# One core, a two-layer graph network: denominators on 32 columns, an earlier mask and a new order of groups

## The chip, the cores and the metric

The kernel runs on one core of one Trainium2 chip. The metric is the device time of one execution in microseconds (us). TensorE (PE) multiplies matrices, with the weights loaded by a second stream (PEld); VectorE (DVE) and ScalarE (ACT) work element by element; GpSimd (POOL) does small element work and issues the gathers; SyncE (SP) issues the plain DMAs. Each engine and each DMA queue takes its instructions in the order in which they were built.

## The reference

The input is `x` (32 images x 512 nodes x 256 features, f32) and `adj` (32 x 512 x 512, 0 or 1, about 3% ones). Two layers follow, each a graph step and then a feed-forward step, with a layer norm ahead of each and a residual sum after it.

```
L0 graph   h = x W_msg;  out = relu(x W_upd + (adj^T h) / max(degree, 1) + bias)
L0 ffn     t = max over d of (x[d] + Wt[:, d]) + bt          # 1024 features, "tropical"
           trop = piecewise linear function of t;  cls = gelu(x Wc + bc);  g = sigmoid(x Wg + bg)
           out = (g * trop + (1 - g) * cls) Wd + bd
L1 graph   four heads of 64:  h = x W[head]
           w[i, j] = leaky_relu(src[i] + dst[j]) where adj[i, j] is 1, else minus infinity
           out = softmax over j of w[i, j], times h;  relu, + h, layer norm per head
L1 ffn     softmax over 64 slices per head of 8; tokens = weighted sums of x over the nodes / weights' sum;
           a short state-space scan over the 64 tokens, forwards and backwards; back to nodes; out projection
```

## The kernel before

The large matmuls are in f32. In the profile one f32 matmul of the program is two TensorE instructions, a transpose is one. P = 128 partitions, N = 512 nodes, NT = 4 tiles of 128 nodes, D = 256.

**The built order.** The code is a set of generators. Every `yield` ends a step, and `woven(a, na, b, nb)` takes steps of two generators in the ratio na : nb. The building layer may still move an instruction in its engine's order where nothing depends on it, so the order on each engine is fixed when the program is built. Tiles come from rings (`bufs`); a tile that takes the place of an older one waits until that one's last reader is done.

**L0** (`layer0_sorted`). The images are cut into 4 segments of 8. `convs` runs the graph step of a segment image by image (`conv_in`, `conv_out`: names `ph`, `pu`, `pm`, `lnpa`), then `put_in_order` sorts the segment's 4096 nodes by how many of their largest features can matter for the tropical maximum. Beside the first segment, `features` sorts the 1024 feed-forward features by the shape of their function: it scatters rows to DRAM, loads them back in order (`wraw`, `fld`, `wd`) and turns them on TensorE (`wtp`, L358) into `table` and the weights. The sorted nodes are 32 tiles of 128 with caps 24, 9, 7, 6, 5, 5, 5, then five of 4, four of 3, seven of 2, nine of 1: a tile with cap k gathers one row of `table` per node as a start (`best`) and k - 1 more (`rows`, L576), and takes the maximum on VectorE (L579). Group g of a segment holds tiles g, g + 8, g + 16 and g + 24. `sums(s, g)` is that gathering; `mixed(s, g)` is the classical product, gate and piecewise function (`clsp`, `gatep`, L599; `tz`, L606; L601 to L617); `down(s, g)` is the last product (`po`, L626) and the store to `x2s`. `feed_forwards` runs the first group's `sums` alone and then weaves `mixed` of a group with `sums` of the next; all of it is woven with the convolutions of the next segment (`ahead`), which end with the set-up of L1's constants.

**L1** (`layer1_plain`). For image b, `prepare(b)` gathers x, loads `adj` (`ai`), makes `a` (bf16) and two sums per row on ScalarE (L1102, L1103), turns `a` on TensorE (`maskp`, L1160) and copies it to `mask` (L1161); it norms and turns x (`x3T`), forms the heads (`hp`, L1131) and three factors of the weights; one of them, `own`, is written to DRAM and read back as a row on all partitions for each head (L1151). `weigh` makes the weights of two heads and one j-tile on VectorE: `att` = max(own, other) * mask (L1170). `attention(b)` then has 8 turns: a pair of heads q (outer loop) and a tile j of 128 source nodes (inner loop). A turn multiplies `att` with the heads' values (numerator, `avp`) and with the column of `hv` that holds the factor of the denominator, broadcast to 64 columns (`adp`):

```
for dst, col, n in ((pv, 0, HO), (pd, HO, 1)):
    for k in range(2):
        h = 2 * q + k
        vals = hv[:, j, h, col : col + n]
        nc.tensor.matmul(dst[k * HO : (k + 1) * HO, :], vals if n > 1 else vals.to_broadcast([P, HO]),
                         weighed[b, h, j], start=j == 0, stop=j == NT - 1)
```

At the end of a pair ScalarE copies both sums from PSUM (L1215, L1216), and a turn later `back` transposes them (`dp`, `bp`, L1185) and divides on VectorE (L1187 to L1189). `norm` finishes the image inside the next image's turns.

`mixer(g)` does the feed-forward step of two images: `slices` (`x4T`; the logits `lgp`, L1289; the softmax; the token sums `yTp`, L1301; `swp`, L1306, whose copies add up `rn`), `tokens` (`uTp`, L1320, and `rnp`, L1323), `scan`, `unslice` (`outp`, L1518). Each `yield n` of the mixer earns n * PACE steps of `ahead`, the attentions with `prepare` of the image after them; WANTED is the sum of the n in one group, and TURNS and STEPS count the steps of an attention and a `prepare`. So attention work stands between the mixer's steps, and the numbers at the yields say how much of it stands where.

Of the kernel before, what the change touches and what calls it, by code (L numbers as in the profile page):

```python
# [96 lines left out]
def layer0_sorted(tc, ident, eps, x, adj, w, x2s, ranks, over, following):  # L97
# [29 lines left out]
    with ExitStack() as ctx:  # L127
# [80 lines left out]
        def features(raw):  # L208
# [141 lines left out]
            nc.sync.dma_start(wd, placed[:, :, D : 2 * D])  # L350
            wtT = rtile("wtT", [P, DC, FFN])
# [169 lines left out]
        def feed_forwards():  # L521
# [110 lines left out]
            groups = [(s, g) for s in range(len(x2s)) for g in range(NG)]  # L632
# [22 lines left out]
        with tc.tile_pool(name="r0", bufs=1) as raw:  # L655
            first = iter(lambda: next(ahead), 0)
            next(first)
            bounds(raw)
            for _ in woven(first, SEG * 10, features(raw), 50):
                pass  # L660
# [175 lines left out]
def layer1_plain(tc, ident, eps, x2s, ranks, adj, w, out, over, ps):  # L836
# [23 lines left out]
    TURNS = AP * (NT + 1) + 3  # L860
    STEPS = 15
    WANTED = 62
    AHEAD = 3
    ATT = 2 * (AHEAD + 2)
# [6 lines left out]
    with ExitStack() as ctx:  # L871
# [167 lines left out]

        yield True  # L1040
# [38 lines left out]
        def prepare(b):  # L1079
# [10 lines left out]
            a, raw = [], []  # L1090

            def load(t):
                raw.append(sb.tile([P, N], I32, tag="ai", name=f"ai{b}_{t}", bufs=2))
                nc.sync.dma_start(raw[t], adj[b, t * P : (t + 1) * P, :])

            load(0)
            load(1)
            yield
            for t in range(NT):
                n = b * NT + t  # L1100
                a.append(sb.tile([P, N], BF16, tag="a", name=f"a{b}_{t}", bufs=3))
                nc.scalar.activation(a[t], raw[t], AF.Identity, accum_out=edges[:, 0, n : n + 1])  # L1102
                nc.scalar.activation(raw[t], raw[t], AF.Square, accum_out=edges[:, 1, n : n + 1])  # L1103
                if t + 2 < NT:
                    load(t + 2)
                if t == 1:
                    mask = sb.tile([P, NT, N], BF16, tag="mask", name=f"mask{b}")
                    yield
                if t:
                    turn_edges(b, t - 1, a[t - 1], mask)  # L1110
                    yield
                if t == 2:

                    hv = sb.tile([P, NT, AH, HE], F32, tag="hv", name=f"hv{b}")
                    xn = hv.rearrange("p t h e -> p (t h e)")[:, : NT * D].rearrange("p (t d) -> p t d", t=NT)
                    normed(xt, xn, f"c{b}")
                    nc.gpsimd.tensor_add(xt, xt, beta.unsqueeze(1).to_broadcast([P, NT, D]))
                    yield
            turn_edges(b, NT - 1, a[NT - 1], mask)
            yield  # L1120
# [28 lines left out]
            own = [wide("own", f"own{b}_{h}", AH + 1) for h in range(AH)]  # L1149
# [6 lines left out]

        def turn_edges(b, t, a, mask):
            pt = ps.tile([P, NT, P], BF16, tag="any", name=f"maskp{b}_{t}")
            for j in range(NT):
                nc.tensor.transpose(pt[:, j, :], a[:, j * P : (j + 1) * P], identb)  # L1160
            nc.vector.tensor_copy(mask[:, :, t * P : (t + 1) * P], pt)  # L1161
# [11 lines left out]
        def attention(b):  # L1173

            mask, ht, hv, other, own = ready[b]
            xt = xs[b]
            av = sb.tile([P, NT, AH, HO], F32, tag="av", name=f"av{b}", bufs=1)
            turns = [(q, j) for q in range(AP) for j in range(NT)]

            def back(q, vT, dT):  # L1180

                bt, dt = psum("pv", f"bp{b}_{q}"), psum("pv", f"dp{b}_{q}")
                for src, dst in ((dT, dt), (vT, bt)):
                    for t in range(NT):
                        nc.tensor.transpose(dst[:, t * P : (t + 1) * P], src[:, t * P : (t + 1) * P], ident)  # L1185
                rs = sb.tile([P, NT, 2], F32, tag="rs", name=f"rs{b}_{q}")
                nc.vector.tensor_scalar_max(rs, dt.rearrange("p (t h e) -> p t h e", t=NT, h=2)[:, :, :, 0], 1e-30)  # L1187
                nc.vector.reciprocal(rs, rs)
                nc.vector.tensor_mul(av[:, :, 2 * q : 2 * q + 2, :], bt.rearrange("p (t h e) -> p t h e", t=NT, h=2),  # L1189
                                     rs.unsqueeze(3).to_broadcast([P, NT, 2, HO]))  # L1190

            def begin(b):
                if b < B and (b, 0, 0) not in weighed:
                    for q, j in turns[:AHEAD]:
                        weigh(b, q, j)

            begin(b)
            behind = None
            for i, (q, j) in enumerate(turns):
                if j == 0:  # L1200
                    pv, pd = psum("pv", f"avp{b}_{q}"), psum("pv", f"adp{b}_{q}")
                if i + AHEAD < len(turns):
                    weigh(b, *turns[i + AHEAD])

                for dst, col, n in ((pv, 0, HO), (pd, HO, 1)):
                    for k in range(2):
                        h = 2 * q + k
                        vals = hv[:, j, h, col : col + n]
                        nc.tensor.matmul(dst[k * HO : (k + 1) * HO, :], vals if n > 1 else vals.to_broadcast([P, HO]),  # L1209
                                         weighed[b, h, j], start=j == 0, stop=j == NT - 1)  # L1210
                for k in range(2):
                    weighed[b, 2 * q + k, j] = None
                if j + 1 == NT:
                    vT, dT = wide("att", f"avT{b}_{q}", ATT), wide("att", f"adT{b}_{q}", ATT)
                    nc.scalar.copy(dT, pd)  # L1215
                    nc.scalar.copy(vT, pv)  # L1216
                    behind = q, vT, dT
                yield
                if unfinished and i != 2:
                    next(unfinished[0], None)  # L1220
                    yield
                    if i > 2:
                        unfinished.pop()
                if j == 0 and behind:
                    back(*behind)
                    behind = None
                    yield
            if b + 1 in ready:
                begin(b + 1)
            back(*behind)  # L1230
            yield
            unfinished.append(norm(b, av))
# [39 lines left out]
        def slices(b, j, yT, rn):  # L1272
# [12 lines left out]
            yield 1  # L1285
            for t in range(NT):
# [10 lines left out]
                yield 4 if t + 1 == NT else 1  # L1297
# [14 lines left out]
        def tokens(g, yT, rn, uT):  # L1312
# [3 lines left out]
            for k in range(KC):  # L1316
                for i in range(P // C):
                    half, h = slice(i * C, (i + 1) * C), k * (P // C) + i
                    for c in range(DC):
                        nc.tensor.matmul(uv[half, k], wfxT[:, c, h * C : (h + 1) * C], yT[:, c, h],  # L1320
                                         start=c == 0, stop=c == DC - 1)
                    for j in range(GB):
                        nc.tensor.matmul(nv[half, k, j, :], rn[:, j, k : k + 1].to_broadcast([P, C]), ident[:, half],  # L1323
                                         start=True, stop=True)
# [9 lines left out]
        def scan(g, uT):  # L1334
# [123 lines left out]
            yield 6  # L1458
# [65 lines left out]
        def mixer(g):  # L1524
# [6 lines left out]
            yield 2  # L1531
# [659 lines left out]
```

## Time and profile before

| | us |
|---|---|
| median of three timed runs | 4762.39 (4759.25 to 4769.2) |
| profiled execution | 4746.8 |
| its span, first to last instruction | 4745.1 |
| first `clsp` of L0's first group | 352 |
| end of L0's last `po` | 2530 |
| first `avp` of L1 | 2565 |
| first and last group's `uTp` begin | 2683 and 4672 |

The profile is of one execution. Busy time of an engine is the union of its instructions' spans; a wait is idle time of an engine, put down to what ended it. In a row of groups stand the line, the engine and operation, the tiles written and read, the shape (for a matmul rows*columns of the array that it uses, then the output's shape), the count, then busy us, mean ns of one, idle us ahead of it and what ended that. A matmul's span holds its latency; how fast matmuls follow each other is read from their starts. Mean granted TensorE clock: 0.95.

### The profile page before, as it was taken

The page shows a single profiled execution, that of the slowest core. Times are in us where ns is not written, and L with a number is a line of the kernel's source. Part 1 is how long each engine was busy: PE and PEld are TensorE (multiplying, and loading weights), DVE is VectorE, ACT ScalarE, POOL GpSimd, SP SyncE. Part 2 cuts the span into 40 slices and gives each one's busy share as a digit, 9 for nine tenths or more (in the row PEclk, how much of TensorE's full clock was granted, in tenths as well). Part 3 has the DMA queues.
Part 4 walks back from the last instruction along what each step waited for, and adds up shares of the span by engine and source line. Part 5 has one row for each costly group of instructions (what it writes and reads, how often), then busy time and mean ns, then how long its engine had stood idle before and what let it go on. Part 6 is the DMA issues. An engine that isn't in the chain of part 4 may idle for free. (4 is left out here: it accounts for less than half of the span.)

```text
span 4745.1 us, 56724 instructions
## 1 busy us (share of the span) xinstructions
PE 4179.0 (88%) x19415; PEld 2594.1 (55%) x19415; DVE 3403.5 (72%) x7296; ACT 2325.0 (49%) x4852; POOL 1701.6 (36%) x2027
## 2 busy tenths in 40 slices
PE   5666989888998899889997999999999999999997
PEld 4444555555555565555554555555555555555555
DVE  6568778887787877777766877667676776666773
ACT  2335555455554556555655544444444444444432
POOL 2356443554435544353323222222222222222220
PEclk8878999999999999989998999999999999999999
DMA  4456443554335543464322111111111111111100
GB/s 122 158 186 197 136 130 113 193 177 134 121 125 179 184 131 115 124 230 158 121 90 83 38 48 54 50 45 54 49 41 39 45 56 50 54 45 50 43 10 19
DMA packets 235104, 474.12 MB, mean 100 GB/s; under 512 B 38300, under 2 KB 114076, under 8 KB 234805
## 3 DMA queue, kind: packets, MB, share of 16 engines
q0 software_dynamic: 80256, 282.38, 18.7%
q1 hardware_dynamic: 154548, 188.02, 12.5%
q8 instruction: 155, 2.54, 0.2%
q14 instruction: 145, 1.18, 0.1%
HBM read 413.16 MB, written 57.16 MB: 99 GB/s over the span
## 5 line engine op out<-in xcount | busy, mean ns | idle before, releaser
L599 PE MATMUL clsp<-xnT,wc 128*128 128x512 f32 x1024 | 508.5, 614 | 48.4 <-ACT cls L601 33.6
L599 PE MATMUL gatep<-xnT,wg 128*128 128x512 f32 x1024 | 499.0, 606 | 6.5 <-ACT gate L601 5.8
L626 PE MATMUL po<-wd,acc 128*128 128x256 f32 x2048 | 468.3, 387 | 28.8 <-DVE xs L628 21.2
L626 PEld LDWEIGHTS po<-wd,acc 128*128 128x128 f32 x2048 | 393.5, 194 | 111.5 <-DVE xs L628 33.5
L1170 DVE SCALAR_TENSOR_TENSOR att<-own,other,mask 128x512 f32<-128x512 f32 x512 | 389.8, 802 | 8.9 <-DMA own<-ownd 6.3
L613 DVE SCALAR_TENSOR_TENSOR acc<-past,fld,acc 128x512 f32<-128x512 f32 x448 | 351.1, 786 | 46.2 <-ACT past L612 37.1
L579 DVE SCALAR_TENSOR_TENSOR best<-rows,xs,best 128x1024 f32<-128x1024 f32 x212 | 272.7, 1288 | 137.8 <-ACT best L573 80.6
L1209 PE MATMUL avp<-att,hv 128*64 128x512 f32 x1024 | 356.9, 619 | 4.1 <-DVE att L1170 4.0
L1209 PE MATMUL adp<-att,hv 128*64 128x512 f32 x1024 | 356.1, 600 | 0.0
L412 PE MATMUL pm<-h,adj 128*128 128x257 f32 x1024 | 280.7, 416 | 85.1 <-DVE xs L628 30.5
L608 ACT ACTIVATE acc<-tz,fld 128x512 f32<-128x512 f32 x256 | 198.9, 778 | 298.7 <-PE tz L606 298.5
L576 POOL DMA_INDIRECT rows<-table,xs x212 | 258.8, 1221 | 209.3 <-DVE best L579 155.5
L599 PEld LDWEIGHTS gatep<-xnT,wg 128*128 128x128 f32 x1024 | 195.6, 194 | 240.7 <-issue 196.8
L612 ACT ACTIVATE past<-tz,fld 128x512 f32<-128x512 f32 x448 | 292.2, 692 | 67.5 <-DVE acc L613 66.8
L1289 PE MATMUL lgp<-wsl,x4T 128*128 128x512 f32 x512 | 265.9, 654 | 56.4 <-ACT x4T L1074 53.9
L599 PEld LDWEIGHTS clsp<-xnT,wc 128*128 128x128 f32 x1024 | 183.6, 195 | 186.4 <-issue 115.3
L412 PEld LDWEIGHTS pm<-h,adj 128*128 128x128 f32 x1024 | 203.8, 208 | 142.0 <-issue 72.1
L601 ACT ACTIVATE cls<-clsp,fld 128x512 f32<-128x512 f32 x256 | 176.9, 691 | 158.7 <-PE clsp L599 72.7
L601 ACT ACTIVATE gate<-gatep,fld 128x512 f32<-128x512 f32 x256 | 175.8, 687 | 125.9 <-PE gatep L599 107.0
L1301 PE MATMUL yTp<-sw,x 128*128 128x512 f32 x512 | 231.9, 599 | 6.1 <-DVE sw L1296 4.2
L1518 PE MATMUL outp<-v,swT 128*128 128x256 f32 x1024 | 227.6, 381 | 0.0
L531 POOL DMA_INDIRECT xs<-rows_of,order x128 | 138.6, 1083 | 247.5 <-DVE acc L613 101.5
(597 smaller groups left out, 9086.2 us busy)
## 6 DMA issues: line engine op xcount, KB each, us to landing
adji<-in_adj SPq DMA_DIRECT2D x128, 256.0 KB
ai<-in_adj SPq DMA_DIRECT2D x128, 256.0 KB
own<-ownd SPq DMA_DIRECT2D x128, 256.0 KB
rows_of<-keep SPq DMA_DIRECT2D x32, 550.0 KB
x<-in_x SPq DMA_DIRECT2D x32, 512.0 KB
x2s<-xs SPq DMA_DIRECT2D x32, 512.0 KB
out<-x SPq DMA_DIRECT2D x32, 512.0 KB
rows<-table,xs POOLq DMA_INDIRECT x212
```

Source lines behind the costliest of these rows:

```text
L412: nc.tensor.matmul(pm[:, : D + 1], a[:, i, t * P : (t + 1) * P], h[:, i, :], start=i == 0, stop=i == NT - 1)
L576: nc.gpsimd.indirect_dma_start(out=row, out_offset=None, in_=table, in_offset=bass.IndirectOffsetOnAxis(ap=idxs[:, k : k + 1].bitcast(U32) ...
L579: nc.vector.scalar_tensor_tensor(m, row, vals[:, k : k + 1], m, ALU.add, ALU.max)
L599: nc.tensor.matmul(pf, wf[:, c, f * P : (f + 1) * P], xnT[:, c, :], start=c == 0, stop=c == DC - 1)
L601: nc.scalar.activation(o, pf, fn, bias=fld[:, f, bf : bf + 1], scale=1.0 if fn == AF.Gelu else 0.5)
L612: nc.scalar.activation(r, z, AF.Relu, bias=fld[:, f, AT + b : AT + b + 1])
L613: nc.vector.scalar_tensor_tensor(y, r, fld[:, f, CH + b : CH + b + 1], y, ALU.mult, ALU.add)
L626: nc.tensor.matmul(po[:, :D], acc[f][:, t * P : (t + 1) * P], wd[:, f, :], start=f == 0, stop=f == FC - 1)
L1170: nc.vector.scalar_tensor_tensor(e, own[h], other[:, j, h : h + 1], mask[:, j, :], ALU.max, ALU.mult)
L1209: nc.tensor.matmul(dst[k * HO : (k + 1) * HO, :], vals if n > 1 else vals.to_broadcast([P, HO]), weighed[b, h, j], start=j == 0, stop=j == ...
L1289: nc.tensor.matmul(pf, xnT[:, c, t * P : (t + 1) * P], wsl[:, c, :], start=c == 0, stop=c == DC - 1)
L1301: nc.tensor.matmul(py, xn[:, t, c * P : (c + 1) * P], sw[:, t, :], start=t == 0, stop=t == NT - 1)
```

## The change

In L1's attention the turns go over j outside and over the pair q inside, and both pairs' numerators stay open. The denominators of all four heads are one PSUM tile with 32 columns (output partitions) per head, made after the second pair of each j. They are transposed back once per image instead of once per pair, at the image's end, after three ScalarE copies. Weights are made 2 turns ahead instead of 3, the ring of `own` has 6 places instead of 5, and that of `att` 11 instead of 10.

`tokens` makes all `uTp` first and then all `rnp`. A generator of its own, `masks`, makes the masks, with tiles of uint8 instead of bf16, and transposes each tile one step later after its ScalarE passes. Image 0's masks are made at the end of L1's set-up, which runs inside L0. Four yields of the mixer grow by 1 (two in `slices`, which runs twice per group, one in `scan` and one ahead of `tokens`), with WANTED, TURNS and PACE to match.

In L0, `features` has six more yields between the loads of the sorted rows and their transposes, with 56 for 50 in its weave. The groups of a segment run from 7 to 0 instead of from 0 to 7.

```diff
@@ features
             nc.sync.dma_start(wd, placed[:, :, D : 2 * D])
+            for _ in range(6):
+                yield
             wtT = rtile("wtT", [P, DC, FFN])
@@ feed_forwards
-            groups = [(s, g) for s in range(len(x2s)) for g in range(NG)]
+            groups = [(s, g) for s in range(len(x2s)) for g in reversed(range(NG))]
...
-            for _ in woven(first, SEG * 10, features(raw), 50):
+            for _ in woven(first, SEG * 10, features(raw), 56):
@@ layer1_plain
-    TURNS = AP * (NT + 1) + 3
+    TURNS = AP * NT + 6
     STEPS = 15
-    WANTED = 62
-    AHEAD = 3
-    ATT = 2 * (AHEAD + 2)
+    WANTED = 68
+    AHEAD = 2
+    ATT = 2 * (AHEAD + 2) + AP + 1
+    HW = P // AH
...
+        def masks(b, bank="any"):
...
+                    mask = se.tile([P, NT, N], mybir.dt.uint8, tag="mask", name=f"mask{b}")
...
+        yield from masks(0, "mm")
         yield True
...
-            own = [wide("own", f"own{b}_{h}", AH + 1) for h in range(AH)]
+            own = [wide("own", f"own{b}_{h}", AH + 2) for h in range(AH)]
@@ attention
-            turns = [(q, j) for q in range(AP) for j in range(NT)]
+            turns = [(q, j) for j in range(NT) for q in range(AP)]
...
+            pv = [psum("pv", f"avp{b}_{q}") for q in range(AP)]
             for i, (q, j) in enumerate(turns):
...
                 for k in range(2):
+                    h = 2 * q + k
+                    nc.tensor.matmul(pv[q][k * HO : (k + 1) * HO, :], hv[:, j, h, :HO], weighed[b, h, j],
+                                     start=j == 0, stop=j == NT - 1)
+                if q + 1 == AP:
+                    if j == 0:
+                        pd = psum("pv", f"adp{b}")
+                    for h in range(AH):
+                        nc.tensor.matmul(pd[h * HW : (h + 1) * HW, :], hv[:, j, h, HO:].to_broadcast([P, HW]),
+                                         weighed.pop((b, h, j)), start=j == 0, stop=j == NT - 1)
                 yield
...
+            dT = wide("att", f"adT{b}", ATT)
+            nc.scalar.copy(dT, pd)
+            vT = [wide("att", f"avT{b}_{q}", ATT) for q in range(AP)]
+            for q in range(AP):
+                nc.scalar.copy(vT[q], pv[q])
+            yield
+            dt = back(dT, "dp")
+            rs = sb.tile([P, NT, AH], F32, tag="rs", name=f"rs{b}")
...
@@ slices, scan, mixer
-            yield 1
+            yield 2
             for t in range(NT):
...
-                yield 4 if t + 1 == NT else 1
+                yield 5 if t + 1 == NT else 1
...
-            yield 6
+            yield 7
...
-            yield 2
+            yield 3
             tokens(g, yT, rn, uT)
@@ tokens
                         nc.tensor.matmul(uv[half, k], wfxT[:, c, h * C : (h + 1) * C], yT[:, c, h],
                                          start=c == 0, stop=c == DC - 1)
+            for k in range(KC):
+                for i in range(P // C):
+                    half = slice(i * C, (i + 1) * C)
                     for j in range(GB):
                         nc.tensor.matmul(nv[half, k, j, :], rn[:, j, k : k + 1].to_broadcast([P, C]), ident[:, half],
                                          start=True, stop=True)
```

## The prediction, made before the changed kernel ran

> **What bounds the kernel now.** I read the page's busy times first, then busy time by stage, then the groups of TensorE (PE) instructions inside the long second stage, then single turns on the timeline, then the waits. The page and the stages:
>
> ```profile
> PE 4179.0 (88%) x19415; PEld 2594.1 (55%) x19415; DVE 3403.5 (72%) x7296; ACT 2325.0 (49%) x4852; POOL 1701.6 (36%) x2027
> ...
> core 0: us, PE busy (x) PEld busy (x) DVE busy (x) ACT busy (x) POOL busy (x), PEclk, DMA share, GB/s
> 282.00:352.00 70.00, 47.28 (x173) 35.14 (x173) 45.63 (x138) 24.38 (x48) 53.02 (x69) 0.81 0.74 234
> 352.00:2078.00 1726.00, 1516.66 (x5704) 979.74 (x5702) 1357.18 (x2763) 951.08 (x1653) 833.62 (x1113) 0.96 0.47 151
> 2078.00:2530.00 452.00, 414.07 (x1471) 250.84 (x1471) 322.56 (x470) 253.51 (x387) 153.05 (x144) 0.96 0.39 125
> 2530.00:2683.00 153.00, 124.37 (x531) 63.38 (x533) 114.35 (x226) 76.01 (x227) 58.14 (x46) 0.89 0.26 81
> 2683.00:4566.00 1883.00, 1768.15 (x9938) 1040.97 (x9934) 1305.57 (x2827) 874.89 (x2224) 508.93 (x385) 0.97 0.15 47
> ```
>
> Up to 282 us L0's first segment is convolved; 282 to 352 is the first group's `sums`; 352 to 2530 are L0's 32 groups; 2530 to 2683 is L1's start; 2683 to 4566 is L1's steady part (14 of its 16 mixer groups, 134.5 us each). There PE is busy 1768 of 1883 us (94%), VectorE (DVE) 69%, ScalarE (ACT) 46%. So PE time taken out of the steady part should come back; in L0 PE is at 88% and DVE at 79%, so neither alone decides. PE's groups in the steady part:
>
> ```profile
> L1209 PE MATMUL adp<-att,hv 128*64 128x512 f32 x896 | 313.4, 599 | 0.0
> L1209 PE MATMUL avp<-att,hv 128*64 128x512 f32 x896 | 312.7, 616 | 0.0
> L1289 PE MATMUL lgp<-wsl,x4T 128*128 128x512 f32 x448 | 237.2, 662 | 55.6 <-ACT x4T L1074 53.1 <-DVE mask L1161 2.4
> L1323 PE MATMUL rnp<-ident,rn 128*64 128x64 f32 x448 | 39.9, 224 | 20.7 <-DVE rn L1309 20.7
> L1185 PE MATMUL dp<-ident,adT 128*128 128x128 f32 x224 | 33.8, 274 | 0.0
> ```
>
> The attention's denominator `adp` costs as much PE time as its numerator `avp`, and its weights are one column repeated 64 times. The two named waits are the only large ones. How one turn runs:
>
> ```profile
> 3312.78 1.03 PE L1209 MATMUL adp<-att,hv 128*64 128x512 f32 x4
> 3313.74 1.09 PE L1073 MATMUL x3T13p<-ident,hv 128*128 128x128 f32 x8
> 3314.76 1.08 PE L1209 MATMUL avp<-att,hv 128*64 128x512 f32 x4
> 3315.67 1.03 PE L1209 MATMUL adp<-att,hv 128*64 128x512 f32 x4
> 3316.63 0.70 PE L1301 MATMUL yTp<-sw,x 128*128 128x512 f32 x1
> ```
>
> A head is two instructions, so x4 is one pair of heads. From 3314.76 to 3315.67 the `avp` pair takes 0.91 us, where the full-width 128x512 matmul starts one every 0.43 us: four instructions in the time of two, so the two 64-column halves run side by side. `adp` to the next 128-column matmul is 0.96 us, 0.86 of stream and 0.10 for the change of width.
>
> **L1's attention.** Before, 32 images x 8 turns = 256 `adp` pairs at 0.86 us = 220 us. After, 128 groups of four heads, 32 columns each. No matmul of 32 columns is in this trace. Bounds: all four at once (as two are now), 0.86 us a group; two at a time, 1.72. I take 0.86, since the pair shows no loss at all: 110 us, a gain of 110. Widths change more often (64, 32, 128): counted in the two built orders, 773 changes against 651 after the first `avp`; 122 x 0.10 = +12. `dp` drops from 8 to 4 transposes an image at 0.109 us: 128 x 0.109 = -14. In the built order 116 of the 128 fours stand whole, and slightly fewer pairs are torn than before; summing both orders at the row durations, torn ones run alone, gives 1887 and 1770 us of PE after the first `avp`: -117 in all, so the last -5 is tearing. How much arrives? PE has 6% of visible idle; that idle is latency of the mixer chain, which attention steps cover and will cover a little less. I take 0.9, **-105** (bounds -60, if half is handed to DVE, and -117). Also gone are 32 ACT copies of 0.58 us and 64 small DVE operations; neither engine is the bound: nothing.
>
> A rule of the Trainium skill speaks against taking the pair's lossless overlap to four: "TensorE: Matmul & The Clock Gate", Part 3 (Packing small matmuls), measured 2.38 times for three 32-column tiles of 512, so each runs at 0.79 of its share. By that page a four is an estimated 1.08 us, 128 x 0.22 = 28 us of the gain go, and the forecast would be 4620 instead of 4592. No run here shows a 32-column tile.
>
> **New waits of the attention.** Turns now go over j with both pairs inside, so all four `own` rows serve until turns 7 and 8. The ring grows from 5 to 6: the next image's heads 2 and 3 take the slots of heads 0 and 1, free after turn 7, and are needed in that image's turn 2. These two loads wait on SP; behind them in that queue are the next adjacency tiles and the output stores. DVE's `att`, and behind it softmax and norm work, waits for the landing. Now `att` waits for `own` 6.3 us in all. `att` also runs 2 turns ahead, not 3; PE waited only 4.1 us for it in all. Masks become uint8: `mask` copies take 412 ns for 128x512 while DVE's f32 operations of that size take 680 to 800; without the short form +0.27 us x 128 = 35 us of DVE, on an engine with 31% free. `att` is at the f32 pace already (802 ns), so I leave it. Together **+12** (bounds 0 and +60: some 2 us an image). The back-transposes at an image's end wait for three ACT copies (1.8 us); mixer work covers them, except in L1's start: +2 there.
>
> **Tokens grouped.** All `uTp` first, 32 instructions at 0.109 us = 3.5 us of work that does not need `rn`: the 20.7 us wait is covered; the next late thing is ACT's copy to `scale`, 0.6 us, unchanged. **-16** (0 to -21).
>
> **Yields and pace.** The extra yield before `lgp` puts an attention step over the `x4T` copy that cost 53.1 us in 10 places. What is shifted can wait elsewhere: **-20** (0 to -53).
>
> **First masks beside L0.** L1's start shows the mask chain:
>
> ```profile
> 2534.92 0.61 PE L1160 MATMUL maskp<-identb,a 128*128 128x128 bf16 x4 [5.41 <-ACT a L1102]
> 2541.86 0.61 PE L1160 MATMUL maskp<-identb,a 128*128 128x128 bf16 x4 [4.29 <-ACT a L1102]
> 2549.21 6.28 PE L1131 MATMUL hp<-wa,x3T 128*128 128x264 f32 x16 [2.82 <-ACT x3T L1074]
> ```
>
> Eight ACT passes at 0.63 us and their accumulator reads at 0.19 (6.6 us) interleave with the norm. They, 4 SP loads (ahead of later `x2s` stores on that queue), 16 transposes at 0.06 and 4 DVE copies go into L0's last segment, where ACT is at 56% and DVE at 71%; their four PSUM tiles come from the pair that `po` turns over in, each for one 0.4 us copy. The other chain, gather, norm, `x3T`, `hp`, `own`, stays. -8, with the +2 above **-6** (0 to -12).
>
> **L0's weights.** In the waits before 352 us:
>
> ```profile
> PE wtp L358 <- DMA wraw<-sorted_rows: 14.0, 1, 14.0
> ```
>
> PE stood 14.0 us with convolution steps behind it. Six yields put some 8 conv steps ahead of it. `table` is written at 199 and first read at 289, so nothing is late. **-12** (0 to -14).
>
> **L0's order of groups.** Group 0 gathers 27 table rows (caps 24, 4, 2, 1), group 7 five (4, 3, 1, 1). The first `sums` runs 70 us with no mixing beside it, 27 DVE passes at 1.29 us = 35 of them. With five, 22 x 1.29 = 28 us of DVE go; the conv steps ahead of the first `clsp` in PE's order remain. Also group 0's mixing (first `clsp` at 352, the next group's at 437: 85 us, where groups 3 to 6 take 67 to 70) loses its tail of rows. I take 26 + 12 = **-38** (0 to -60). Price: a heavy `sums` now runs beside all four segments' mixing, not three. Heavy neighbours took 74 to 78 us and their successors 86 to 88 against some 68, and L0's last segment has only 52 us a group. **+15** (0 to +35).
>
> **Sum.** -105 + 12 - 16 - 20 - 6 - 12 - 38 + 15 = -170. The profiled execution took 4746.8 us (span 4745.1 and 1.7 around it): 4577. The median of the three timed runs, 4762.4, lies 15.6 above; I carry that over: **4592 us**.
>
> **Rivals.** (1) Four 32-column streams do not run together: two at a time give the 110 back, 4702. For it: no such row in the trace. Against: pairs start 7 ns apart and finish together. (2) PE falls, the period does not follow: DVE's order or the mixer's chain holds it. For: DVE 69% in order, PE's residual waits all on DVE or ACT. Half of the L1 terms (-105, -16, -20) lost, +70: 4662. (3) Slower: the wait for `own`. At L1's start the first `own` load is issued at 2557.7 and its `att` starts at 2563.7, so one exposed load costs at most 6.0 us; in all 31 hand-overs 186 us, which beats the 170: 4778. It decides from 5.5 us an image. Against: one to two turns, some 10 us of steady pace, lie between release and use.
>
> **How the numbers follow.** My case 0.72, with its own bounds 4540 (the full 117: 12 more; the yields worth 38: 18; L0's order 22 better) to 4650 (`att` waits of 60: 48; the yields worth half: 10); (1) 0.10; (2) 0.14; (3) 0.04. The range leaves out (1) and (3) and reaches past (2): 4540 to 4685. A measurement here tells about 0.2% (9.5 us) from no change. Faster: all but (3) and a corner where (1) and (2) meet: 0.94; same 0.02; slower 0.04.
>
> **What would show it.** Right: `adp` 128*32 x1024 with half its busy time, some 180 us, four starts within 25 ns; the steady period near 125 us; `rnp`'s wait gone; first `clsp` near 315 us; `wtp`'s wait gone; L0's last two groups longer than 52 us. Wrong: `adp` near 350 us (1); PE's share of the steady part well under 94% with new waits on `att` or `x4T` (2), or `att` waiting on DMA `own` (3).

## The result: 1.4% faster, and the profile after

Two effects stood against each other: by the profiles, L0 ends 42 us later than before and L1 takes 93 us less.

| | before | after | the forecast |
|---|---|---|---|
| median of the timed runs, us | 4762.8 | 4694.9 | 4592 (4540 to 4685) |
| ratio, 95% interval | | 0.986 (0.984 to 0.988) | 0.964 |
| span of the profiled execution | 4745.1 | 4693.7 | |
| first `clsp` of L0 | 352 | 338 | 315 |
| L0's 32 groups, first `clsp` to last `po` | 2178 | 2234 | |
| last `po` to the first group's `uTp` | 153 | 164 | |
| 14 steady groups, per group | 134.5 | 126.5 | 125 |
| last two groups (last stage) | 179 | 187 | |

Busy time by stage in the profile of after; the columns are those of the table by stage shown before, and the rows answer to it:

```profile
282.00:338.00 56.00, 39.01 (x154) 29.27 (x153) 36.17 (x112) 29.27 (x54) 42.45 (x59) 0.85 0.72 231
338.00:2103.00 1765.00, 1528.82 (x5696) 982.66 (x5696) 1352.03 (x2766) 948.13 (x1646) 845.21 (x1106) 0.95 0.46 145
2103.00:2572.00 469.00, 420.44 (x1502) 254.20 (x1500) 342.95 (x493) 262.69 (x413) 179.95 (x158) 0.95 0.44 142
2572.00:2736.00 164.00, 129.52 (x495) 54.42 (x497) 110.82 (x212) 65.07 (x196) 59.49 (x46) 0.86 0.21 62
2736.00:4507.00 1771.00, 1661.84 (x9832) 960.34 (x9829) 1306.88 (x2769) 858.70 (x2197) 520.13 (x385) 0.98 0.16 50
```

The steady part lost 112 us (1883 to 1771 in these windows), and PE is busy 1662 of 1771 us (94%, as before): by the prediction's own signs that is its case, with a period near 125. L0 is where the time went back: the first three segments take 1765 us (1726 before) and the last one 469 (452). PE's groups in the steady part, busy us, mean ns, idle ahead and what ended it:

```profile
L1219 PE MATMUL avp<-att,hv 128*64 128x512 f32 x898 | 268.2, 627 | 0.0
L1307 PE MATMUL lgp<-wsl,x4T 128*128 128x512 f32 x448 | 222.7, 631 | 31.9 <-DVE mask L1058 26.2 <-ACT sw L1308 3.3 <-DVE mvc L1100 1.6
L1319 PE MATMUL yTp<-sw,x 128*128 128x512 f32 x448 | 210.6, 609 | 30.3 <-DVE sw L1314 29.6
L1226 PE MATMUL adp<-att,hv 128*32 128x512 f32 x896 | 124.4, 604 | 0.0
L1344 PE MATMUL rnp<-ident,rn 128*64 128x64 f32 x448 | 17.3, 223 | 2.9 <-DVE mu L1265 1.5 <-DVE rn L1327 1.4
```

`adp` is down from 313 to 124 us, and the waits of `lgp` for `x4T` (53) and of `rnp` (21) are gone. In their place stand `lgp` for `mask`, `yTp` for `sw` and smaller ones: all of PE's idle time in the steady part is 109 us, where it was 115. On the timeline, one turn:

```profile
3124.96 1.08 PE L1219 MATMUL avp<-att,hv 128*64 128x512 f32 x4
3125.97 1.06 PE L1226 MATMUL adp<-att,hv 128*32 128x512 f32 x8
3126.96 1.94 PE L1219 MATMUL avp<-att,hv 128*64 128x512 f32 x8
```

The x8 are four heads of two instructions. They take 0.99 us to the next width, 0.86 of it stream, where a pair of 64 columns took 0.86 for two heads. The four starts are 6 to 7 ns apart and the next four come 0.43 us later: four 32-column streams run together without loss. The page cited in the prediction has a gain of 2.38 for three tiles; here four gain 4, the measurement decides, and rival (1) is out.

L0's waits of PE up to the last segment (us in total, times, longest), after and then before:

```profile
PE ph L393 <- DVE xs L630: 58.5, 27, 5.6
PE clsp L601 <- ACT cls L603: 38.3, 23, 4.8
PE clsp L601 <- ACT gate L603: 36.2, 17, 8.0
```

```profile
PE pm L412 <- DVE xs L628: 30.5, 14, 4.3
PE ph L391 <- ACT h L393: 24.2, 14, 4.6
PE clsp L599 <- ACT cls L601: 20.2, 18, 6.2
```

The convolution's first product `ph` now waits for VectorE's last sum `xs` of a group 27 times, 2.2 us each. Before, it did so 4 times (8.7 us), and `pm` was the one that waited; all waits for `xs` together grow little, from 65 to 76 us. What grows most are the waits of the classical product and the gate, `clsp` and `gatep`, for ScalarE: 33 us in all before, 94 after. By segments, the groups take 2 us less in the first (its first group is 30 shorter) and 8, 33 and 17 more in the other three. From `clsp` to `clsp`, the groups of the third segment took 87, 68, 75, 65, 70, 65, 59, 69 us before and 76, 71, 70, 70, 75, 70, 78, 81 after.

### The profile page after: what moved, and what is told of

Its sections match the earlier page's. It is cut to its first block, busy times and chain, and to the rows that moved or that the text cites. A ratio compares the mean times of both kernels' runs of the same rounds, so it can differ in the third digit from the quotient of the medians.

```text
span 4693.7 us, 56440 instructions
## 1 busy us (share of the span) xinstructions
PE 4097.9 (87%) x19287; PEld 2514.5 (54%) x19287; DVE 3410.9 (73%) x7232; ACT 2310.3 (49%) x4820; POOL 1747.3 (37%) x2027
## 5 line engine op out<-in xcount | busy, mean ns | idle before, releaser
L601 PE MATMUL clsp<-xnT,wc 128*128 128x512 f32 x1024 | 530.9, 639 | 92.7 <-ACT cls L603 48.5
L628 PE MATMUL po<-wd,acc 128*128 128x256 f32 x2048 | 456.2, 381 | 20.4 <-DVE xs L630 19.9
L1186 DVE SCALAR_TENSOR_TENSOR att<-own,other,mask 128x512 f32<-128x512 f32 x512 | 376.3, 757 | 17.9 <-DMA own<-ownd 16.9
L1219 PE MATMUL avp<-att,hv 128*64 128x512 f32 x1024 | 309.8, 628 | 3.3 <-DVE att L1186 3.3
L414 PE MATMUL pm<-h,adj 128*128 128x257 f32 x1024 | 268.1, 403 | 28.3 <-DVE u L411 18.5
L1307 PE MATMUL lgp<-wsl,x4T 128*128 128x512 f32 x512 | 253.1, 630 | 33.6 <-DVE mask L1058 26.2
L1319 PE MATMUL yTp<-sw,x 128*128 128x512 f32 x512 | 244.1, 617 | 36.8 <-DVE sw L1314 29.6
L1127 POOL DMA_INDIRECT x<-x2s,ranks x128 | 141.3, 1104 | 346.9 <-DVE att L1186 128.5
L617 DVE TENSOR_TENSOR acc<-acc,cls 128x512 f32<-128x512 f32 x256 | 180.6, 707 | 94.3 <-ACT acc L610 88.6
```

The costliest lines, as they stand in the source:

```text
L414: nc.tensor.matmul(pm[:, : D + 1], a[:, i, t * P : (t + 1) * P], h[:, i, :], start=i == 0, stop=i == NT - 1)
L601: nc.tensor.matmul(pf, wf[:, c, f * P : (f + 1) * P], xnT[:, c, :], start=c == 0, stop=c == DC - 1)
L628: nc.tensor.matmul(po[:, :D], acc[f][:, t * P : (t + 1) * P], wd[:, f, :], start=f == 0, stop=f == FC - 1)
L1186: nc.vector.scalar_tensor_tensor(e, own[h], other[:, j, h : h + 1], mask[:, j, :], ALU.max, ALU.mult)
L1219: nc.tensor.matmul(pv[q][k * HO : (k + 1) * HO, :], hv[:, j, h, :HO], weighed[b, h, j], start=j == 0, stop=j == NT - 1)
L1307: nc.tensor.matmul(pf, xnT[:, c, t * P : (t + 1) * P], wsl[:, c, :], start=c == 0, stop=c == DC - 1)
```

## The experiments

The experiments ran on several chips, each time beside the kernel before on the same chip (medians 4751 to 4761), so kernels are compared by their ratios to it. Stages come from each one's profile, in us. "Steady" is from the first to the fifteenth group's `uTp`; the eleven kernels with the L1 of after lie between 1758 and 1775 there, ten of them between 1766 and 1775. The last `po` varies by 13 us among the eight kernels with e1_fwd's L0, and by 16 among the four with few rows first and 16 steps ahead. "Many first" is the old order of groups, in which a segment starts with the group of 27 gathered rows; "few first" is the new one.

| run | ratio (95%) | first `clsp` | last `po` | steady |
|---|---|---|---|---|
| before | 1 | 352 | 2530 | 1884 |
| after | 0.986 (0.984, 0.988) | 338 | 2572 | 1771 |
| e1_fwd | 0.978 (0.976, 0.980) | 350 | 2543 | 1774 |
| e2_rev | 1.010 (1.008, 1.011) | 346 | 2586 | 1884 |
| e3_noyield | 0.988 (0.986, 0.990) | 344 | 2588 | 1772 |
| e4_late | 0.987 (0.985, 0.989) | 337 | 2580 | 1769 |
| e5_wide | 0.986 (0.983, 0.988) | 345 | 2537 | 1802 |
| e6_yield | 0.979 (0.976, 0.982) | 350 | 2542 | 1767 |
| e7_tokens | 0.982 (0.980, 0.985) | 348 | 2536 | 1785 |
| e8_actmask | 0.974 (0.971, 0.977) | 348 | 2537 | 1757 |
| e9_oldatt | 1.002 (1.001, 1.004) | 349 | 2535 | 1891 |
| e10_slope | 0.976 (0.974, 0.978) | 350 | 2531 | 1758 |
| e11_revlead | 0.991 (0.989, 0.993) | 307 | 2597 | 1758 |
| e12_fwdlead | 0.986 (0.984, 0.988) | 307 | 2565 | 1770 |
| e13_rev_quarter | 0.972 (0.969, 0.974) | 331 | 2508 | 1766 |
| e14_fwd_quarter | 0.961 (0.958, 0.964) | 335 | 2457 | 1767 |
| e15_rev_row | 0.966 (0.964, 0.968) | 337 | 2481 | 1775 |
| e16_fwd_row | 0.957 (0.954, 0.960) | 343 | 2433 | 1768 |
| e17_rev_phase | 0.980 (0.979, 0.982) | 307 | 2548 | 1772 |
| e18_old_split | 0.994 (0.993, 0.996) | 350 | 2543 | 1865 |

### L0: each of its edits undone

```diff
# e1_fwd, from after
-            groups = [(s, g) for s in range(len(x2s)) for g in reversed(range(NG))]
+            groups = [(s, g) for s in range(len(x2s)) for g in range(NG)]
# e2_rev, from before: the opposite edit alone
# e3_noyield, from after
-            for _ in range(6):
-                yield
             wtT = rtile("wtT", [P, DC, FFN])
# ... and 50 for 56 in the weave again
# e4_late, from after
-        yield from masks(0, "mm")
```

> The changed kernel with L0's groups in the old order (many rows first). Theory A (the new order of groups is what makes L0's 32 groups 56 us longer, 2234 against 2178 from the first clsp to the last po): the groups return to about 2180 us, the first clsp goes from 338 to about 352 or 360, and the time is about 4660 us (4695 - 54 + 20), faster than the changed kernel. Theory B (the feature yields, or the first masks, lengthen the groups, and the order gains as forecast): the groups stay near 2230, and the time is 4715 to 4735.

> The kernel before with nothing changed but L0's order of groups (few rows first). The prediction's own terms for this edit are -38 and +15: 4762 - 23 = 4739. Theory A: the first clsp comes 15 to 25 us earlier and the 32 groups take some 55 us more: about 4795. Theory B: 4739 or less.

> The changed kernel without the six yields in L0's features (and the weight of that stream back at 50). The prediction's term: the 14.0 us wait of wtp returns, +12: 4707. Theory A: the same, 4700 to 4709, the groups unchanged within 5 us. Theory B (the yields push convolution steps into the groups' time): the groups shorten by 20 us or more and the time is below 4685.

> The changed kernel with the first image's masks made in L1's start again (still one byte an element). The prediction's term: L1's start grows, +6 to +8: 4701 to 4703. Rival: the masks in L0's last segment (469 us against 451 or so before) cost more there than they save, and the time is 4680 to 4690 with the last segment near 452.

Of L0's edits only the order of groups has a price that can be told from nothing: put back, it gives 0.8% (0.986 to 0.978, some 38 us); alone in the kernel before it costs 1.0% (45 us). Theory A holds in both, except that the first `clsp` moved by 12 and 6 us, less than A had. The six yields took `wtp`'s wait away (13.2 us in e3_noyield, none in after) and the first `clsp` came 6 us earlier; in the whole time that can't be told from nothing. The place of the first masks is worth nothing either: L1's start takes 164 us in both.

### L1: what the steady part's 112 us consist of

```diff
# e5_wide, from e1_fwd: sums on 64 columns, two PSUM tiles, two transposed sets
-                        nc.tensor.matmul(pd[h * HW : (h + 1) * HW, :], hv[:, j, h, HO:].to_broadcast([P, HW]),
+                        nc.tensor.matmul(pd[h // 2][h % 2 * HO : (h % 2 + 1) * HO, :],
+                                         hv[:, j, h, HO:].to_broadcast([P, HO]),
# ... the copies and the transposes to match
# e6_yield, from e1_fwd: mixer's yields 1, 4, 6, 2 again
-    WANTED = 68
+    WANTED = 62
# ...
# e7_tokens, from e1_fwd: rnp inside the loop of uTp again
# e8_actmask, from e1_fwd
-                nc.vector.tensor_copy(mask[:, :, t * P : (t + 1) * P], pt)
+                nc.scalar.copy(mask[:, :, t * P : (t + 1) * P], pt)
```

> The kernel of e1_fwd with the weight sums on 64 columns a head again (two PSUM tiles, two transposed sets), everything else of the new attention kept. Out of the prediction's first term: 112 fours in the 14 steady groups become 224 pairs, +112 x 0.86 = 96, and 112 more transposes x 0.109 = 12: +108 us of PE in the steady part. Theory A (PE sets the period, 0.9 or more arrives): the steady part goes from 1774 to 1871 to 1882 us, the whole kernel 110 us above e1_fwd. Theory B (other waits set the period): half of it, 1828.

> The kernel of e1_fwd with the mixer's old yields (1, 4, 6, 2 in place of 2, 5, 7, 3, and 62 in place of 68 in the pace). The prediction's term is 20 us for all of it (bounds 0 and 53). Theory A: the wait of lgp for x4T returns and the steady part is some 18 us longer, 1792. Theory B (removed waits only move to the next late thing): steady part 1774 within 6 us, with the same 109 us of idle PE under other names.

> The kernel of e1_fwd with the token products in the old order (uTp and rnp by turns). The prediction's term is 16 us. Theory A: rnp waits for rn again, about 1.4 us a group, and the steady part is 14 to 20 us longer. Theory B (the extra attention step ahead of the tokens already covers the wait): within 4 us, and rnp's wait stays under 5 us in all.

> The kernel of e1_fwd with the copy of each mask tile from PSUM on ScalarE in place of VectorE: 112 x 0.68 = 76 us leave VectorE in the steady part and some 70 go to ScalarE (49% busy there). Theory A (the waits for VectorE that are left on PE, 26.2 us of lgp and 11.4 of maskp on mask, are real delays): the steady part falls by 20 to 38 us, to 1736 to 1754, faster than e1_fwd. Theory B (they are only names of slack that lies elsewhere): 1774 within 6 us, other waits in their place.

e5_wide is the surprise: without the 32 columns the steady part is only 28 us longer, half of even theory B's 54. The steady part of e1_fwd and then of e5_wide, in the columns of the table by stage:

```profile
2703.00:4477.00 1774.00, 1664.49 (x9830) 962.29 (x9828) 1312.59 (x2769) 858.90 (x2197) 521.45 (x385) 0.98 0.16 50
2699.00:4501.00 1802.00, 1730.80 (x9946) 1010.94 (x9945) 1291.00 (x2799) 874.10 (x2226) 515.03 (x385) 1.00 0.16 49
```

With the wide sums PE is busy 1731 us, 66 more than in e1_fwd, but idle only 71 where e1_fwd idles 109. So most of the steady part's gain is there without the 32 columns, and most of what they take out of PE comes back as waits: mainly for VectorE's `mask` (`lgp` and `maskp`, 5 us in e5_wide and 38 in e1_fwd) and for the mixer's `yT` (`oTp`, 1 and 11).

Old yields (e6_yield): theory B, the same within what can be told, and the wait of `lgp` for `x4T` does not come back (2.5 us). With the new turns the yields are not needed for it. Nor are the new turns needed with the yields and the new masks: in e9_oldatt below it is 11 us of the 53. Old token order (e7_tokens): 11 us longer, with `rnp` waiting 3.1 us in all, as much as in e1_fwd (2.9). The 11 are PE's own: products and sums by turns take 4.0 us a group from first `uTp` to last `rnp`, grouped ones 2.9. e8_actmask: 17 us shorter, between the theories (A 20 to 38, B 6); the waits for `mask` went and `yTp`'s for `sw` grew from 30 to 59. The 17 are as much as the steady part varies with the same L1, but in the whole time its runs (4625 to 4640) lie below those of e6_yield on the same chip (4646 to 4668). It is the fastest version here that does all of the work, at 0.974, ahead of the kernel before by 2.6% and of after by 1.2%.

### Whose gain it is, and what more PE time returns

```diff
# e9_oldatt, from e1_fwd: the whole of attention() as before, with its TURNS, a lead of 3, a ring of 10
+            turns = [(q, j) for q in range(AP) for j in range(NT)]
# ...
# e10_slope, from e1_fwd: sums made for j == 0 only, the other three j left out (and 1.0 as the sum's lower bound)
+                        if j == 0:
+                            nc.tensor.matmul(pd[h * HW : (h + 1) * HW, :], hv[:, j, h, HO:].to_broadcast([P, HW]),
+                                             e, start=True, stop=True)
# e11_revlead, from after; e12_fwdlead, from e1_fwd
-    LEAD = 16
+    LEAD = 4
```

> The kernel of e1_fwd with the attention of the kernel before (one pair of heads after the other, sums on 64 columns, a lead of 3 turns), the new masks, yields and token order kept. e5_wide has its steady part at 1802 us with the heads two and two inside each j; the kernel before has 1884. Theory A (the gain of the new attention lies in its order of turns, not in its 32 columns): 1850 to 1880 here. Theory B (masks, yields and tokens gave it): 1800 to 1815 here.

> The kernel of e1_fwd with the weight sums left out for three of the four j (the division uses a part of the sum): 84 of 112 fours at 0.99 us leave PE in the steady part, 83 us, with two changes of width each in part. Theory A (PE's work is no longer what sets the period; e5_wide returned 28 of 99 us): the steady part falls by some 20 to 30 us, to 1745 to 1755. Theory B (PE sets it, the prediction's 0.9): by 75, to 1700.

> The changed kernel with 4 steps of the next segment's convolution ahead of the first sums in place of 16. Theory A (these 16 steps, not the gathered rows, set the first clsp, which came at 338 instead of the 315 of the prediction): the first clsp comes near 305 us. Theory B (the gathers and VectorE's passes set it): it stays at 330 or later. The steps that are put off are done beside the groups: the end within 10 us of the changed kernel, either way.

> The kernel of e1_fwd (many rows first) with 4 steps of convolution ahead of the first sums in place of 16: the pair of e11_revlead. Theory A (with few steps ahead the 27 rows of the first sums lie bare): the first clsp is 25 to 35 us later than in e11_revlead (with 16 steps it is 12 later: 350 against 338). Theory B: 12 us later as with 16 steps. The whole kernel near 4660.

Old attention with all else new: 1891 us, 7 more than the kernel before. So the masks, yields and grouped tokens together returned nothing by themselves (`rnp` waits its 20 us here, with `uTp` grouped), and from 1891 the new order of turns gives 89 (to e5_wide's 1802) and the 32 columns 28. The 89 belong to the order with all that came along: the lead of 2 turns, the first weights of the next image made inside the last turns, and the back-transposes at the image's end. By ratios the chain is 1, 1.002, 0.986, 0.978, and 0.986 with L0's new order. e10_slope prices what is left: another 83 us out of PE return some 16, one fifth, and 0.2% of the whole time. With the same L1, e11_revlead's steady part is as short (1758), so the fifth is rough; what is sure is that the 75 us of theory B did not come. Waits of the mixer grew instead: `yTp` for `sw` from 30 to 44 us, `yp` for `mix` from 5 to 21. PE is busy in most of every stretch, but it no longer sets the period.

e11 and e12: with 4 steps ahead the first `clsp` comes at 307 in both orders. Theory A for e11 holds. For e12 both theories fall, since each had the many rows delay the first `clsp`: at 4 steps they do not delay it at all. They delay the first group's later steps: it takes 61 us with few rows and 110 with many (54 and 84 with 16 steps).

### Why the order costs: passes, gathers or the place of the steps

```diff
# e13_rev_quarter, from after; e14_fwd_quarter, from e1_fwd: three quarters of each pass left out
-                        nc.vector.scalar_tensor_tensor(m, row, vals[:, k : k + 1], m, ALU.add, ALU.max)
+                        nc.vector.scalar_tensor_tensor(m[:, : FFN // 4], row[:, : FFN // 4], vals[:, k : k + 1],
+                                                       m[:, : FFN // 4], ALU.add, ALU.max)
# e15_rev_row, from after; e16_fwd_row, from e1_fwd: one gathered row a tile, used for all its passes
+                        if k == 1:
# e17_rev_phase, from after
-    LEAD = 16
+    LEAD = 10
# e18_old_split, from e9_oldatt: a step between PE's and VectorE's half of back, TURNS + 2
+                yield
                 rs = sb.tile([P, NT, 2], F32, tag="rs", name=f"rs{b}_{q}")
```

> The changed kernel (few rows first) with VectorE's pass over each gathered row on a quarter of its columns (256 of 1024; the rest of the row is left out of the maximum); every row is still gathered. 212 passes lose about 0.95 us each. Until now the last po of L0 comes at about 2580 us with few rows first and 2537 with many first, 43 apart. Theory A (the passes are what the groups wait for): the two orders come within 10 us of each other or few-first leads, since only its gain at the start is left. Theory B (the gathers): still 35 or more apart.

> The pair of e13_rev_quarter: the kernel of e1_fwd (many rows first) with passes of a quarter of the columns. Theory A: its last po within 10 us of e13_rev_quarter's. Theory B: 35 us or more earlier than there. In both theories earlier than the 2537 of the full passes.

> The changed kernel (few rows first) with one gathered row a tile: the further passes use that row again (120 of 212 gathers are left out, the passes stay full). Theory A (passes): the two orders stay some 35 to 45 us apart at the last po. Theory B (gathers): within 10 us of each other.

> The pair of e15_rev_row: the kernel of e1_fwd (many rows first) with one gathered row a tile. Theory A: last po 35 to 45 us earlier than in e15_rev_row, near 2537. Theory B: within 10 us of e15_rev_row, both earlier than 2537.

> The changed kernel (few rows first) with 10 steps of convolution ahead of the first sums: half an image (an image has 12 steps) from the phases of 16 (last po at 2572 to 2588) and 4 (2597). Theory A (the place within the group at which an image of convolution starts sets the 43 us): the waits of ph and po for xs between 420 and 2000 us fall from 74 (62 with 4 steps) to below 35, and the last po comes at 2560 or earlier. Theory B (not the phase): first clsp near 322, the last po between 2575 and 2600.

> The kernel of e9_oldatt with VectorE's half of the back-transposition (rs and av) one step after PE's half. In e9_oldatt VectorE stands 101 us of the steady part at rs for PE's dp, with all its later work queued behind; in the new attention 0.2 us. Theory A (this wait is what the new order of turns took away): the steady part falls from 1891 to 1800 to 1825. Theory B (the turns' order itself, two heads' pairs by turns, gives it): above 1870.

Passes of a quarter leave the orders 51 us apart, one row a tile 48 (last `po`). Theories A and B of these four both say that one of them closes the distance, and neither does: neither VectorE's passes alone nor the gathers alone make the price of the order, though both cost time in either order. e17 moves where in a group an image of convolution begins, by half an image, and L0 ends at 2548, against 2572 to 2588 with 16 steps and 2597 with 4. The waits of `po` for `xs` are 19.4 us and `ph` has left the list, but `pm` has taken its place (up to the last segment):

```profile
PE pm L414 <- DVE xs L630: 57.8, 21, 5.3
PE clsp L601 <- ACT cls L603: 23.1, 15, 4.2
PE lnpa L60 <- ACT xna L56: 21.3, 9, 4.2
PE pm L414 <- DVE u L420: 21.1, 9, 4.0
PE po L628 <- DVE xs L630: 19.4, 22, 2.8
```

Theory A's numbers are met, but not its mechanism: the waits for `xs` only changed their place. What fell are the waits of `clsp` and `gatep` for ScalarE. Up to the last segment they are 32 to 34 us in the nine kernels with many rows first and 16 steps (the kernel before and the eight with e1_fwd's L0), 92 to 98 in the four with few first and 16 steps, and 42 in e17. PE's idle time from the start to the last `po` tells the same: 374 to 387 us, 410 to 426, and 383 in e17; its busy time differs by 26 us at most, without such a pattern.

So the steps of convolution that are built ahead, with the same work in all, move L0's end by 24 to 49 us, about the size of the order's price. That it is their place in a group, and not their number, is likely but not shown. e17 against e11 speaks for the place: the first `clsp` comes at 307 in both, and L0's end is 49 us apart. Against it, 16 and 4 steps are one whole image apart and share the place, and still L0's end differs by 22 us with many rows first (2543 and 2565). Nor are e17's 32 groups shorter than those of after (2240 us, 2234): they carry more of the convolution, and the 31 us earlier start makes the gain. Many first with 10 steps was not run.

Counted in the trace, most groups of after hold exactly one image of convolution (64 instructions of `ph`, `pm`, `pu`), the group that carries the 27-row sums 28 and the next one 100; before, they hold 48 to 88. In the last two segments the price also sits in the groups with heavy sums: before, 59 and 69 us ended the third segment and 52, 48, 61 the fourth; after, 78 and 81, and 61, 62, 66. What holds them stays open.

The other open cause, e18: VectorE's wait of `rs` for `dp`, in the whole run of before and in the steady part of e9_oldatt (us in total, times, longest):

```profile
DVE rs L1187 <- PE dp L1185: 105.5, 34, 5.4
```

```profile
DVE rs L1203 <- PE dp L1201: 100.7, 36, 5.4
```

In e18's whole run:

```profile
DVE att L1186 <- DMA own<-ownd: 65.8, 14, 5.1
DVE rs L1204 <- PE dp L1201: 61.8, 34, 3.7
```

Put a step apart, the wait fell from 103.5 to 61.8 us in the whole run, and the steady part from 1891 to 1865: 26 of the 89 us. Neither theory's number is met (A 1800 to 1825, B above 1870). The wait is part of the cause. How much of it is not settled, since e18 brought a wait of its own: VectorE's `att` stood 65.8 us for `own`, once in each steady group, where e9_oldatt has 9.4 and e5_wide 11.3. The other 63 us belong to the new order of turns and what came along with it, in a way that these runs do not split; the gap between e18 and e5_wide stands largely ahead of `maskp` on PE (a 51 us wait in e18, 2 in e5_wide).

## Why the prediction was wrong

The direction was right, the time was 4695 instead of 4592, 10 us above the range. Its steps, in its order:

- **L1's attention, -105.** The stream was read rightly: 0.86 us a four, one more change of width. "How much arrives? I take 0.9" is the step that failed: about 0.3 arrives (28 us of the 96 of stream in the steady part, 112 x 0.86; 36 us in the whole time), and some 0.2 of the next 83 (e10_slope). PE at 94% was taken for a bound; the 6% of idle were taken for latency that attention would cover only a little less. Between e5_wide and e1_fwd PE's idle time rose from 71 to 109 us, at `mask` and at the mixer's `yT`. That the mixer's steps keep their count of attention steps while each of these became shorter, and so covers less, fits this; no run shows it by itself. Rival (2) had a period that does not follow PE, at 0.14.
- **New waits, +12.** The same paragraph described the new order of turns and gave it only a price. With what came along it was the largest gain, 89 us in the steady part (1.6% of the whole). Evidence of a part of it was in the profile before, where VectorE stood 105 us in 34 waits at `rs` for `dp`, with all its later work queued behind. The prediction named no wait of VectorE for PE. `att`'s wait for `own` grew from 6.3 to 16.9 us, well inside the bounds, and the copy of a mask went from 412 to 678 ns, the +0.27 us as estimated.
- **Tokens, -16; yields, -20.** Tokens gave 11, not from the covered wait but from PE's shorter run. The yields gave nothing that can be told; the wait for `x4T` goes with the new turns alone and nearly so without them. The two waits named there were not the only large ones: `yp` stood 17.4 us for `mix`. The sum for the steady part, 14/16 of -129 or -113, met the measured -112 by luck, with every term off.
- **First masks, -6.** Nothing. The start takes 164 us with the masks early or late (after and e4_late), where before it took 153. POOL's `hv` (L1162) now starts 6.5 us after `hp` is done, behind gathers, a norm and the sum with `beta` of later images; before it was 0.7. That does not explain the longer start: in e9_oldatt `hv` starts 7.7 us after `hp` and the start takes 154. What does stays open; with the new attention it is 154 to 165.
- **Features, -12.** 6 at the first `clsp`; the wait itself was read rightly.
- **L0's order, -38 and +15.** The gain came, though not where it was put: the first `clsp` 6 to 12 us earlier instead of 26, since 16 steps of convolution are built ahead of it and it does not need the rows; the first group 30 shorter (84 to 54) instead of 12. The price is the second failed step and decides the miss: groups 2 to 32 took 2180 us where they took 2093, +86 against +15 (0 to +35). With the gains of this edit set against it, a net cost of 38 to 45 us remains (e1_fwd, e2_rev) where the sum had a gain of 23. It was priced from the same groups' durations in the old order, as if each pairing of sums and mixing kept its cost wherever it stood. In PE's waits the price shows at `clsp` and `gatep` for ScalarE, 33 us before and 94 after; why stays open in part, as said above. Without this edit the kernel runs at 0.978, which is 4658 on the first chip, inside the range.
- **The end**, not in the sum. +8 us in the last stage, with PE's busy time unchanged (144 and 145 us) and a granted clock of 0.85 instead of 0.91; not separated.

## What to carry to other kernels

Before work is taken from a busy engine, ask how much of its idle time is latency that this very work covers: 94% busy returned three tenths of what was taken out, then some two. Read the waits of the other in-order engines as well: 100 us stood on VectorE while PE's list looked nearly clean, and splitting that one wait gave 26. In a build that weaves two streams by counting steps, a new order of loops also moves the places at which the streams meet; six steps more or fewer ahead moved L0's end here by 24 to 49 us, with the same work.

## What the runs showed of the hardware

**A long idle stretch costs more than its length.** After a wait of 3.4 us, PE went on at half its pace:

```profile
3194.59 0.39 PE L1057 MATMUL maskp<-identb,a 128*128 128x128 bf16 x4
3198.34 3.68 PE L1307 MATMUL lgp<-wsl,x4T 128*128 128x512 f32 x4 [3.36 <-DVE mask L1058]
```

```profile
3189.00:3198.30 9.30, 5.97 (x24) 2.69 (x20) 6.03 (x12) 3.44 (x7) 6.66 (x6) 1.00 0.33 97
3198.30:3202.00 3.70, 3.66 (x6) 1.17 (x6) 3.70 (x5) 3.08 (x8) 2.88 (x3) 0.54 0.23 48
```

Four `lgp` start 0.9 us apart instead of 0.43, at a granted clock of 0.54, so the wait of 3.36 cost an estimated 5.2. In L1 of before and after, the mean granted clock of the next 2 us was below 0.8 after all 18 waits above 3 us ahead of a full 128x512 f32 matmul (3.1 to 6.6 us), and after 1 of 30 waits between 0.8 and 2 us. The Trainium skill's "TensorE: Matmul & The Clock Gate", Part 1, gives an idle window of about 3.4 us for this; the runs agree.

**VectorE held by POOL.** A sum of two 128x512 tiles that takes 0.68 us took 2.73 while POOL added a 128x1024 tile (before):

```profile
2980.28 2.75 POOL L1282 TENSOR_TENSOR x<-x,outb 128x1024 f32<-128x1024 f32 x1 [3.52 <-ACT x L1064]
```

```profile
2980.86 2.73 DVE L1455 TENSOR_TENSOR mix<-mix,back 128x512 f32<-128x512 f32 x1
```

It ended 0.55 us after POOL's, and so did this sum in 13 other groups. The Trainium skill's "SBUF — State Buffer", section "SBUF: two separate sides", calls the port pair of the two engines an exclusive lock; these rows look like that.
